# Another order of a period's small products, the mixing as 64x32 parts, and longer instruction periods, in a fused attention and feed-forward kernel

## The chip, the cores and the metric

The kernel runs on one core of one Trainium2 chip. The metric is device time in microseconds of one execution. Single executions of the kernel before agree within 0.25 us (1237.48 to 1237.73). A profiled execution gives the trace that is read here; its times are counted from the start of its span. L12 is line 12 of the kernel. The engines are TensorE (PE, its weight loads PEld), VectorE (DVE), ScalarE (ACT), GpSimd (POOL) and SyncE (SP), which issues most of the DMA transfers.

## What is computed

The input x is 128 sequences of 32 positions with 512 channels. All of it is float32. Cut to what matters:

```python
# 1. mixing: each sequence has its own 32x32 matrix, drawn from 16, that mixes its positions
h = einsum('bct,bcd->bdt', x, W[condition])
# 2. attention: clip, layer norm with affine on q and k, 32 heads of 16, ALiBi, causal
q, k, v = split(clip(h @ w_qkv.T, -8, 8))
q, k = layer_norm(q) * q_w + q_b, layer_norm(k) * k_w + k_b
s = where(causal, q @ k.T * 16**-0.5 + slopes * rel, -inf)
x = x + (softmax(s) @ v) @ w_out.T
# 3. adapters: each sequence has its own 512x512 matrix, drawn from 8
a = einsum('bsi,boi->bso', x, weight[adapter_ids])
# 4. feed-forward with a routed branch, layer norm, residual
shared = relu(a @ up) ** 2 @ down
routed = ((a @ fc1) @ expert) * sum(top2(a @ gate)) @ fc2
x = x + layer_norm(shared + routed) * gamma + beta
```

## The kernel before

The 4096 rows are cut into 32 tiles of 128 rows, which are four sequences. Every tile passes through a chain of steps that stretches over several periods; a loop over t, from 2 to 33, runs one period per turn and works on several tiles at once (L775 to L826). Two tiles make a pair, and the up product of the feed-forward is done for a pair: even t runs the eight blocks of up for pair t/2 - 1, odd t runs the eight quarters of down for the pair's two tiles. What stands before the loop (L662 to L767) brings tiles 0 to 3 to where the loop takes them up.

The steps that matter here, by the tile's name in the profile:

- mix (pxc, L290): the mixing. The four 32x32 matrices of a tile stand on the diagonal of a 128x128 block matrix blk, zero elsewhere (blend, L278); four products of 128x128 with 128 columns give xcT, channels by rows, copied out of the bank by ScalarE (L295).
- project (pqkv, L307): three products of 128 rows with 512 columns, for q, k, v.
- turn and scale: q and k are transposed. For tiles 0 to 3 TensorE does it (pt, L365); from tile 4 on VectorE transposes 32x32 blocks (L346), and DMAs through DRAM finish the swap (T_qk). ScalarE then applies the affine to the keys (L386) and to the queries (L400); VectorE makes kx, the keys of each head with zeros for the other heads (L390).
- scores (psc, L414): 32 products that use 64 rows and 32 columns of the array, 128 columns wide, into two banks; VectorE adds the bias (L424) and takes the maximum mx (L435), POOL subtracts it (L436), ScalarE exponentiates (L441).
- share and flip: VectorE sums (den, L446), POOL divides (L449), VectorE transposes (pT, L457).
- weigh (po, L484): the weighted values, 32 products that use 128 rows and 32 columns of the array, 64 columns wide; VectorE transposes the result (aT, L495).
- attend (pw, L506) applies the output matrix; turn_x transposes the new x (T_x), by the same kind of swap.
- adapt (pad, L536): the adapters, 64 products of 128 rows and 32 columns of the array, 128 columns wide; VectorE transposes the result into hT (L541), the input of up and of the routed branch (route, pr, L555).
- up and down (pu, pd, L104), each up block followed by a relu on ScalarE (L585) and a square on POOL (L586).

A float32 product appears in the trace as two records of weight load and two of matmul. So a tile's scores are 64 matmul records, its adapters 128, its mixing 8, its weighted values 64.

Order. TensorE's instructions run in the order of the loop's text: weigh(t), adapt(t - 1), scores(t + 1), route, mix(t + 2), then the projections of t + 2 and the blocks of up or down between them. `after(a, b)` (L77) only orders two instructions of one engine; in adapt and scores it keeps the scores behind the last adapter product. The other engines' instructions are ordered by when the planner of the language expects their inputs, except where `after` fixes it.

Fillers. `fill(i)` (L779) emits block i of up or down and behind it `fill_up(n)`, which emits n empty instructions (NOPs) on TensorE, held between that block and the next product of up or down. n comes from FIRST (t = 2) and SHORT (even t, odd t), spread over the eight blocks: 116 at t = 2, 7 in an even period, 71 in an odd one. In the program's text the products of an even period are 752 instructions (a product counts four), of an odd one 688; with the fillers and 9 semaphore instructions each makes 768.

SyncE's queue. `load_adapters(t)` (L239) issues eight loads of adapter weights; the first of them waits for the cue it is given, the maximum mx of tile t + 1. Behind it on SP stand the load of x for tile t + 3 and the swaps of q, k and x.

Memory. The pool of PSUM has eight banks, handed out in turn; T_qk, T_x, kx, s, pT and aT have one buffer each, xcT, vx and blk two (vx two halves), the adapter weights eight buffers, which is one tile's.

## Time and profile before

| what | value |
|---|---|
| median of three executions | 1237.62 us |
| the profiled execution | 1237.27 us |
| its span | 1235.5 us |
| mean granted TensorE clock | 0.999 |
| DMA traffic | 209.31 MB, mean 169 GB/s |

| one period from tile 16's weighted values on (607.06 us) | us from start to start |
|---|---|
| even period, t = 16 | 37.77 |
| odd period, t = 17 | 37.69 |

| the larger groups | records | busy us | mean ns |
|---|---|---|---|
| pqkv, 128x512 | 768 | 340.3 | 592 |
| pu, 128x256 | 1024 | 228.7 | 379 |
| pd, 128x512 | 496 | 220.4 | 592 |
| pad, 128x128 in 128*32 | 4096 | 118.4 | 273 |
| psc, 64x128 in 64*32 | 2048 | 37.2 | 274 |
| po, 128x64 in 128*32 | 2048 | 35.2 | 220 |
| pxc, 128x128 in 128*128 | 256 | 33.8 | 275 |

How to read it: matmul records overlap each other, and their ends are modelled, so a record's mean length is not what it adds to the time; the distance from one group's first start to the next group's is. Form 64*32 means that a record uses 64 rows and 32 columns of the array, so that eight such parts fit beside each other. A row of the timeline gives the start, the length of the merged stretch, the engine, the line, the operation, the names, the form and the number of records; in brackets, where there was idle time before it, its length and what ended it.

### The profile page before, as it was taken

The page shows a single profiled execution, that of the slowest core. Times are in us where ns is not written, and L with a number is a line of the kernel's source. Part 1 is how long each engine was busy: PE and PEld are TensorE (multiplying, and loading weights), DVE is VectorE, ACT ScalarE, POOL GpSimd, SP SyncE. Part 2 cuts the span into 40 slices and gives each one's busy share as a digit, 9 for nine tenths or more (in the row PEclk, how much of TensorE's full clock was granted, in tenths as well). Part 3 has the DMA queues.
Part 4 walks back from the last instruction along what each step waited for, and adds up shares of the span by engine and source line. Part 5 has one row for each costly group of instructions (what it writes and reads, how often), then busy time and mean ns, then how long its engine had stood idle before and what let it go on. Part 6 is the DMA issues. An engine that isn't in the chain of part 4 may idle for free.

```text
span 1235.5 us, 29216 instructions
## 1 busy us (share of the span) xinstructions
PE 1227.2 (99%) x11614; PEld 790.5 (64%) x11614; DVE 658.3 (53%) x1090; ACT 327.6 (27%) x648; POOL 431.5 (35%) x393
## 2 busy tenths in 40 slices
PE   9999999999999999999999999999999999999998
PEld 4577466675666756567665666746667566675765
DVE  2975655646456464563646546465564645646222
ACT  2432223222222313133222232222322222231211
POOL 4543333433423424334243333333333242332410
PEclk9999999999999999999999999999999999999999
DMA  9745553435545345544355543455443554434630
GB/s 289 220 166 197 206 205 147 156 121 196 205 174 177 102 175 197 200 162 140 139 185 206 184 155 125 155 206 205 150 154 124 190 204 176 176 110 157 209 116 18
DMA packets 93417, 209.31 MB, mean 169 GB/s; under 512 B 11749, under 2 KB 42470, under 8 KB 93286
## 3 DMA queue, kind: packets, MB, share of 16 engines
q1 hardware_dynamic: 89142, 198.39, 45.8%
q0 software_dynamic: 3424, 8.39, 1.9%
q8 instruction: 97, 1.59, 0.5%
q10 hardware_dynamic: 720, 0.66, 0.2%
q14 instruction: 34, 0.28, 0.1%
HBM read 176.47 MB, written 30.93 MB: 168 GB/s over the span
## 4 chain that ended last, share of the span: by engine, by line
PE 99%; DMA 0%; DVE 0%; ACTq 0%; issue 0%; DVEq 0%
PE pqkv L307 27%; PE pu L104 18%; PE pd L104 17%; PE pr L555 10%; PE pad L536 9%; PE pw L506 9%; PE psc L414 3%; PE po L484 3%; PE pxc L290 2%; PE pro L207 1%; PE pd L636 1%; DMA fc_t<-in_fc_w 0%; PE pt L365 0%; PE pe L197 0%; PE pt_x L365 0%; ACTq L124 0%
## 5 line engine op out<-in xcount | busy, mean ns | idle before, releaser
L307 PE MATMUL pqkv<-wqkv_sb,xcT 128*128 128x512 f32 x768 | 340.3, 592 | 0.0
L307 PEld LDWEIGHTS pqkv<-wqkv_sb,xcT 128*128 128x128 f32 x768 | 145.5, 190 | 168.6 <-issue 162.8
L104 PE MATMUL pu<-hT,up_sb 128*128 128x256 f32 x1024 | 228.7, 379 | 0.0
L104 PE MATMUL pd<-down_sb,act 128*128 128x512 f32 x496 | 220.4, 592 | 0.0
L104 PEld LDWEIGHTS pu<-hT,up_sb 128*128 128x128 f32 x1024 | 193.5, 190 | 32.6 <-issue 6.9
L390 DVE TENSOR_TENSOR kx<-T_qk,m_half 128x512 f32<-128x512 f32 x128 | 110.4, 920 | 102.7 <-ACT T_qk L386 102.7
L104 PEld LDWEIGHTS pd<-down_sb,act 128*128 128x128 f32 x496 | 93.2, 190 | 104.7 <-issue 103.6
L471 POOL TENSOR_TENSOR vx<-v,msk 128x1024 f32<-128x1024 f32 x64 | 127.2, 2010 | 56.6 <-DVE v L313 49.9
L586 POOL TENSOR_TENSOR act<-act 128x256 f32<-128x256 f32 x128 | 77.9, 614 | 168.6 <-ACT act L585 168.6
L555 PE MATMUL pr<-rout_sb,hT 128*128 128x256 f32 (+1 forms) x512 | 125.8, 389 | 0.0
L536 PE MATMUL pad<-adw,T_x 128*32 128x128 f32 x4096 | 118.4, 273 | 0.1
L555 PEld LDWEIGHTS pr<-rout_sb,hT 128*128 128x128 f32 x512 | 94.7, 190 | 32.1 <-issue 19.9
L506 PE MATMUL pw<-wout_sb,aT 128*128 128x512 f32 x256 | 115.2, 592 | 0.0
L536 PEld LDWEIGHTS pad<-adw,T_x 128*32 128x32 f32 x4096 | 110.7, 110 | 2.0 <-issue 1.2
L436 POOL TENSOR_TENSOR s<-s,mx 128x1024 f32<-128x1024 f32 x32 | 61.7, 1928 | 143.4 <-DVE top L562 141.8
L446 DVE TENSOR_REDUCE den<-s 128x32 f32<-128x1024 f32 x32 | 39.0, 1220 | 100.5 <-ACT s L441 100.5
L520 POOL TENSOR_TENSOR x<-x,bet_sb 128x512 f32<-128x512 f32 x32 | 40.7, 1272 | 147.1 <-DVE blocks_x L346 144.8
L506 PEld LDWEIGHTS pw<-wout_sb,aT 128*128 128x128 f32 x256 | 48.6, 190 | 60.6 <-issue 60.0
L585 ACT ACTIVATE act<-pu 128x256 f32<-128x256 f32 x128 | 47.2, 379 | 139.6 <-PE pu L104 139.6
L623 POOL DMA_DIRECT2D out<-y x30 | 18.0, 599 | 179.8 <-DVE y L619 93.1
L449 POOL TENSOR_TENSOR s<-s,rden 128x1024 f32<-128x1024 f32 x32 | 61.4, 1919 | 51.2 <-DVE rden L448 48.3
L295 ACT COPY xcT<-pxc 128x512 f32<-128x512 f32 x32 | 18.8, 586 | 201.8 <-PE pxc L290 201.8
(76 smaller groups left out, 1094.5 us busy)
## 6 DMA issues: line engine op xcount, KB each, us to landing
adw<-in_adapt_w SPq DMA_DIRECT2D x256, 512.0 KB, 7.5
away_qk<-blocks_qk SPq DMA_DIRECT2D x28, 512.0 KB, 2.6
T_qk<-away_qk SPq DMA_DIRECT2D x112, 128.0 KB, 2.9
x<-in_x SPq DMA_DIRECT2D x32, 256.0 KB, 9.3
away_x<-blocks_x SPq DMA_DIRECT2D x30, 256.0 KB, 2.7
T_x<-away_x SPq DMA_DIRECT2D x120, 64.0 KB, 2.4
out<-y POOLq DMA_DIRECT2D x30, 256.0 KB, 2.7
wqkv_sb<-in_w_qkvT SPq DMA_DIRECT2D x12, 256.0 KB, 5.3
```

What stands on the lines that cost most here:

```text
L104: ins = nc.tensor.matmul(*args, **kwargs)
L307: nc.tensor.matmul(s["pp", i], lhsT=s["xcT"][:, c, :], rhs=wqkv_sb[:, c, ts(i, D)], start=(c == 0), stop=(c == DC - 1),)
L390: kx = nc.vector.tensor_tensor(out=s["kx"][:, c], in0=k[:, :, c].unsqueeze(2).broadcast_to([P, SEQ, HQ, S]), in1=m_half.unsqueeze(1).unsqu ...
L436: nc.gpsimd.tensor_tensor(out=s["s"], in0=s["s"], in1=mx.unsqueeze(2).broadcast_to([P, H, S]), op=ALU.subtract,)
L449: nc.gpsimd.tensor_tensor(out=s["s"], in0=s["s"], in1=rden.unsqueeze(2).broadcast_to([P, H, S]), op=ALU.mult)
L471: nc.gpsimd.tensor_tensor(out=vx, in0=s["v"][:, ts(half, D // 2)].rearrange("p (h d) -> p h d", d=HD).unsqueeze(2) .broadcast_to([P, H // ...
L506: nc.tensor.matmul(pw, lhsT=s["aT"][:, g].rearrange("p b q -> p (b q)"), rhs=wout_sb[:, g, :], start=(g == 0), stop=(g == 3),)
L520: nc.gpsimd.tensor_tensor(out=s["x"], in0=s["x"], in1=bet_sb, op=ALU.add)
L536: last_pad[:] = [nc.tensor.matmul(pad[ts(g, S), ts(j, P)], lhsT=s["xT"][:, j, c], rhs=s["adw"][c // 2][j][:, c % 2, ts(g, P)], start=(c == ...
L555: nc.tensor.matmul(pr[:, :n], lhsT=hT[:, c, ts(t % GRP, P)], rhs=rout_sb[:, c, ROUT[half] : ROUT[half + 1]], start=(c == 0), stop=(c == DC ...
L585: nc.scalar.activation(a, pu[:, : GRP * P], AF.Relu)
L586: nc.gpsimd.tensor_tensor(out=a, in0=a, in1=a, op=ALU.mult)
```

## The change

- The order of the small products at a period's start becomes scores(t + 1), mix(t + 2), adapt(t - 1), weigh(t). A helper `short` issues them and holds each behind the one before with `after`.
- For tiles from 4 on the mixing is cut: only the two 64x64 diagonal halves of blk are used, as 32 products of 64 rows, 32 columns of the array and 64 columns of data, into two banks, one for each half of the rows; ScalarE copies the two halves of xcT out in two instructions. Tiles 0 to 3 are mixed as before.
- The fillers: FIRST is 3, SHORT is (152, 214), spread over the first seven blocks; behind the eighth there are none.
- In the fifth block of up, the relu is ordered behind the last scaling of the queries (`last_scale`), which stands behind that of the keys on ScalarE.
- The sum den of tile t + 1 is ordered behind the last transposition of the small products on VectorE (`last_head`: aT, or hT at t = 2), and the adapter loads take that transposition as their cue in place of mx.

```diff
--- before.py
+++ after.py
@@ -35,8 +35,8 @@
 ROUT = (0, NE + D // 2, NE + D)
 
 
-SHORT = (7, 71)
-FIRST = 116
+SHORT = (152, 214)
+FIRST = 3
 CLIP = 8.0
 EPS = 1e-5
 NEG = -1.0e30
@@ -92,6 +92,7 @@
 
 
     queue = []
+    shorts = []
 
     def fill_up(n):
 
@@ -104,6 +105,14 @@
         ins = nc.tensor.matmul(*args, **kwargs)
         if queue:
             after(ins, queue.pop())
+        return ins
+
+    def short(*args, **kwargs):
+
+        ins = product(*args, **kwargs)
+        if shorts:
+            after(ins, shorts[-1])
+        shorts[:] = [ins]
         return ins
 
 
@@ -285,14 +294,29 @@
     def mix(t):
 
         s = tiles[t]
-        pxc = bank(f"pxc_{t}")
+        s["xcT"] = w2.tile([P, DC, P], F32, tag="xcT", name=f"xcT_{t}")
+        blk = s["blk"].rearrange("p a b -> p (a b)")
+        if t < 2 * GRP:
+            pxc = bank(f"pxc_{t}")
+            for c in range(DC):
+                nc.tensor.matmul(
+                    pxc[:, ts(c, P)], lhsT=s["x"][:, ts(c, P)], rhs=blk, start=True, stop=True
+                )
+            nc.scalar.copy(s["xcT"].rearrange("p c n -> p (c n)"), pxc)
+            return
+
+        n = P // 2
+        banks = [bank(f"pxc_{t}_{r}").rearrange("p (c n) -> p c n", c=DC) for r in range(2)]
         for c in range(DC):
-            nc.tensor.matmul(
-                pxc[:, ts(c, P)], lhsT=s["x"][:, ts(c, P)],
-                rhs=s["blk"].rearrange("p a b -> p (a b)"), start=True, stop=True,
-            )
-        s["xcT"] = w2.tile([P, DC, P], F32, tag="xcT", name=f"xcT_{t}")
-        nc.scalar.copy(s["xcT"].rearrange("p c n -> p (c n)"), pxc)
+            for g in range(DC):
+                for r in range(2):
+                    short(
+                        banks[r][ts(g, S), c, :n],
+                        lhsT=s["x"][ts(r, n), c * P + g * S : c * P + (g + 1) * S],
+                        rhs=blk[ts(r, n), ts(r, n)], start=True, stop=True,
+                    )
+        for r in range(2):
+            nc.scalar.copy(s["xcT"][:, :, ts(r, n)], banks[r][:, :, :n])
 
     def project(t, i, chunks=range(DC)):
 
@@ -334,7 +358,8 @@
                     after(add, done)
 
     last_flip = []
-    last_pad = []
+    last_head = []
+    last_scale = []
 
     def swap(srcs, name):
 
@@ -397,10 +422,10 @@
             if c == 0 and last_flip:
                 after(kx, last_flip[-1])
         for c in range(DC):
-            nc.scalar.activation(
+            last_scale[:] = [nc.scalar.activation(
                 q[:, :, c], s["raw"][0][:, :, c], AF.Identity,
                 bias=qaff[:, 1, c : c + 1], scale=qaff[:, 0, c : c + 1],
-            )
+            )]
 
     def scores(t):
 
@@ -411,14 +436,12 @@
             for b in range(SEQ):
                 for r in range(2):
                     rows_r = slice(r * P // 2, (r + 1) * P // 2)
-                    psc = nc.tensor.matmul(
+                    psc = short(
                         banks[r][ts(b, S), ts(c, HQ * S)],
                         lhsT=s["T"][rows_r, b, 0, c],
                         rhs=s["kx"][rows_r, c, b].rearrange("p h k -> p (h k)"),
                         start=True, stop=True,
                     )
-                    if last_pad:
-                        after(psc, last_pad.pop())
         s["psc"] = psc
         for r in range(2):
             add = nc.vector.tensor_tensor(
@@ -443,7 +466,9 @@
     def share(t):
         s = tiles[t]
         den = sm.tile([P, H], F32, tag="den", name=f"den_{t}")
-        nc.vector.tensor_reduce(out=den, in_=s["s"], axis=AX.X, op=ALU.add)
+        total = nc.vector.tensor_reduce(out=den, in_=s["s"], axis=AX.X, op=ALU.add)
+        if t > GRP:
+            after(total, last_head[-1])
         rden = sm.tile([P, H], F32, tag="rden", name=f"rden_{t}")
         nc.vector.reciprocal(rden, den)
         nc.gpsimd.tensor_tensor(
@@ -481,7 +506,7 @@
         s = tiles[t]
         po = bank(f"po_{t}")
         for h in range(H):
-            nc.tensor.matmul(
+            short(
                 po[ts(h % 4, S), :].rearrange(
                     "p (e b i d) -> p e i b d", e=DC, b=SEQ, d=HD
                 )[:, h // 8, h // 4 % 2],
@@ -495,6 +520,7 @@
         aT = nc.vector.transpose(
             out=s["aT"].rearrange("p e b q -> p (e b q)"), in_=po
         )
+        last_head[:] = [aT]
         if t == 0:
             after(tiles[2]["stats"], aT)
 
@@ -533,17 +559,17 @@
         for j in range(SEQ):
             for c in range(DC):
                 for g in range(DC):
-                    last_pad[:] = [nc.tensor.matmul(
+                    short(
                         pad[ts(g, S), ts(j, P)], lhsT=s["xT"][:, j, c],
                         rhs=s["adw"][c // 2][j][:, c % 2, ts(g, P)],
                         start=(c == 0), stop=(c == DC - 1),
-                    )]
-        nc.vector.transpose(
+                    )
+        last_head[:] = [nc.vector.transpose(
             out=pairs[t // GRP]["hT"][:, :, ts(t % GRP, P)].rearrange(
                 "p e (j n) -> p e j n", j=SEQ
             ),
             in_=pad.rearrange("p (j e d) -> p e j d", j=SEQ, d=S),
-        )
+        )]
 
     def route(t, half):
 
@@ -582,7 +608,10 @@
                 start=(c == 0), stop=(c == DC - 1),
             )
         a = hp.tile([P, GRP * P], F32, tag="act", name=f"act_{g}_{f}")
-        nc.scalar.activation(a, pu[:, : GRP * P], AF.Relu)
+        relu = nc.scalar.activation(a, pu[:, : GRP * P], AF.Relu)
+
+        if f == FC // 2 and last_scale:
+            after(relu, last_scale.pop())
         nc.gpsimd.tensor_tensor(out=a, in0=a, in1=a, op=ALU.mult)
         pair["acts"].append(a)
         return last
@@ -778,18 +807,19 @@
 
         def fill(i):
             last = up(g, i) if t % GRP == 0 else down(g * GRP + i // 4, i % 4)
-            short = FIRST if t == GRP else SHORT[t % GRP]
+            lack = FIRST if t == GRP else SHORT[t % GRP]
             queue[:] = [last]
-            fill_up(short // 8 + (i < short % 8))
-
+            fill_up(lack // 7 + (i < lack % 7) if i < 7 else 0)
+
+        when(ahead, scores, t + 1)
+        when(two, mix, t + 2)
+        when(t <= NTILE, adapt, t - 1)
         when(here and t > GRP, weigh, t)
-        when(t <= NTILE, adapt, t - 1)
-        when(ahead, scores, t + 1)
         when(ahead, exponent, t + 1)
         if here:
 
 
-            load_adapters(t, tiles[t + 1]["mx"] if ahead else None)
+            load_adapters(t, last_head[-1])
         if t == GRP:
             after(
                 nc.sync.dma_start(out=gam_sb, in_=gamma.broadcast_to([P, D])),
@@ -798,7 +828,6 @@
         when(t + 3 < NTILE, load, t + 3)
         when(t > GRP and t % GRP == 0, finish, t - GRP - 1)
         when(t > GRP, route, t - GRP, 0)
-        when(two, mix, t + 2)
         fill(0)
         when(two, project, t + 2, 0)
         when(ahead, share, t + 1)
```

## The prediction

> **What bounds it now.** I read the page's busy times first, then its chain of waits.
>
> ```profile
> PE 1227.2 (99%) x11614; PEld 790.5 (64%) x11614; DVE 658.3 (53%) x1090; ACT 327.6 (27%) x648; POOL 431.5 (35%) x393
> ...
> PE 99%; DMA 0%; DVE 0%; ACTq 0%; issue 0%; DVEq 0%
> ```
>
> TensorE runs without a hole and the chain never leaves it, so another engine matters only where it comes to be waited for. The time is the sum of what stands in TensorE's order, and a period is read as starts in its timeline. This is tile 16's head (weighted values, adapters, scores, routing, mixing, first block of up):
>
> ```profile
> 607.06 1.10 PE L484 MATMUL po<-vx,pT 128*32 128x64 f32 x64
> 607.98 3.69 PE L536 MATMUL pad<-adw,T_x 128*32 128x128 f32 x128
> 611.60 1.16 PE L414 MATMUL psc<-kx,T_qk 64*32 64x128 f32 x64
> 612.68 2.05 PE L555 MATMUL pr<-rout_sb,hT 128*128 128x264 f32 x8
> 614.57 1.05 PE L290 MATMUL pxc<-blk,x 128*128 128x128 f32 x8
> 615.46 1.89 PE L104 MATMUL pu<-hT,up_sb 128*128 128x256 f32 x8
> ```
>
> From start to start: 0.92, 3.62, 1.08, 1.89, 0.89, together 8.40 us. Everything behind the head (29.3 us, large products back to back) keeps its order.
>
> **The change, part by part.** Durations are of the profiled execution, 1237.27 us (span 1235.5 and 1.8 around it); the median shown, 1237.62, is 0.35 above it.
>
> *Mixing in parts.* Removed: 8 records of 128x128, 0.89 us. Added: 32 matmuls (64 records) of 64x32 with 64 columns. No row has this form, so it is bounded. Below: in the single records of psc, eight parts of the array start a record each per 0.107 us; half the columns would give 64/8 x 0.053 = 0.43. Above: as dear as psc's own, 1.08/64 = 17 ns each, 1.09 us. In between lies what I take. In psc's records the first eight matmuls load at 6.7 ns apart, but the seventeenth loads only 0.435 us after the first: 0.135 to the second record of the first matmul, 0.269 that record, 0.03 on. So sixteen are in flight. With half the columns the second record follows at 0.06, and po's 64-column record is 0.219 long: 0.31 per sixteen, 0.62 for 32, and 0.06 behind the last scores. I take 0.68.
>
> [...]
>
> *Order.* A change of the array's shape costs a drain: from psc's last record to pr's first load 0.20; from po's (64 columns) to the transposes in the prologue 0.15. Before, a head had a drain into po (outside the 8.40), 0.20 after pad and 0.20 after psc. Now it has the same drain into psc, none between psc and mixing, 0.15 after mixing, none between pad and po, 0.15 after po. The new head: psc 1.08 - 0.20 = 0.88; mixing 0.68 + 0.15; pad 3.50 (in the prologue, followed by its own shape, 64.40 to 67.92, 3.52); po 0.92 + 0.11 = 1.03; pr 1.89. Sum 8.13, or **0.27 us less per period**. The periods t = 3 to 29 have all parts: 27 x 0.27 = 7.3. Periods 30 and 31, without mixing, gain 0.05 each.
>
> *The first period.* At t = 2 the head had pad, psc, pxc, and pad covered the wait for tile 3's keys:
>
> ```profile
> 83.27 3.70 PE L536 MATMUL pad<-adw,T_x 128*32 128x128 f32 x128
> 86.90 1.16 PE L414 MATMUL psc<-kx,T_qk 64*32 64x128 f32 x64
> 87.98 1.16 PE L290 MATMUL pxc<-blk,x 128*128 128x128 f32 x8
> 88.98 1.89 PE L104 MATMUL pu<-hT,up_sb 128*128 128x256 f32 x8
> ```
>
> ```profile
> 84.19 2.50 DVE L390 TENSOR_TENSOR kx<-T_qk,m_half 128x512 f32<-128x512 f32 x4 [1.09 <-ACT T_qk L386]
> 87.04 0.72 DVE L541 STREAM_TRANSPOSE hT<-pad 128x512 f32<-128x512 f32 x1 [0.35 <-PE pad L536]
> ```
>
> Now scores come first and wait for kx, ready at 86.69; the chained mixing and adapters queue behind them. Last quarter of the scores 0.27, mixing 0.83, pad 3.63, hT 0.14 + 0.72, start of up 0.1: 92.4 instead of 88.98. The first up needs hT and nothing stands between them here, so this is **+3.3 us**, less perhaps 0.4 if the early scores are done by then. I take +3.0, once (2.0 to 3.6).
>
> *Edits at nothing.* Later the scores' new place needs kx at the period's start. For odd periods kx ended 1.7 us before the next start (680.85, from 676.65, against 682.52); for even ones it ended 0.1 after it, because two relus (L585) went ahead of the scalings:
>
> ```profile
> 639.76 0.38 ACT L585 ACTIVATE act<-pu 128x256 f32<-128x256 f32 x1 [1.25 <-PE pu L104]
> 641.48 0.38 ACT L585 ACTIVATE act<-pu 128x256 f32<-128x256 f32 x1 [1.34 <-PE pu L104]
> 641.76 1.64 ACT L386 ACTIVATE T_qk<-T_qk,lnc 128x128 f32<-128x128 f32 x4
> 643.30 1.64 ACT L400 ACTIVATE T_qk<-T_qk,qaff 128x128 f32<-128x128 f32 x4
> ```
>
> The new order on ACT holds the fifth relu behind the last scaling. The keys can then start after y (638.51) and end near 641.6, kx near 643, 1.9 before 644.83. Behind the held relu wait the later relus, their squares on POOL and pu's banks, each wanted only by the next period. Cover gone, each late microsecond is paid per period. Two ACT copies (0.38 each, by act's row of the same width) replace one of 0.59; xcT is wanted 7 us later. The weight loads now wait on SP for aT or hT (about 7 us into the period) instead of mx (8.3); x's load stands behind them there, and the next adapters start 30 us later, eight issues (4.9 us) and 7.5 to land. den on DVE waits for aT; pT is wanted a period later. hT still has po, the drain and pr (2.9 us) before up.
>
> *Fillers.* In the records they are 71 ns apart, executed while TensorE has some 33 instructions before it. Even periods get 22 behind each of seven blocks, 1.56 us against the block's 1.73. Odd ones get 30 or 31, 2.2 us against 1.72; the three in a row (91 x 0.071 = 6.5) run against 33 instructions (5.4 us) and two blocks (3.4): 2.4 us stay in hand. Cost nothing; with no lead at all, 3 x 0.45 us per odd half.
>
> Sum: -7.3 - 0.1 + 3.0 = -4.4 on 1237.27, with 0.35 for the median: 1233.2. A part of a tenth per period for waits of the mixing's own (its bank, its data) I leave in: 27 x 0.02. **1233.7.**
>
> **Rivals.** *Blocks of instructions in the way (slower).* TensorE's stream comes in 16 KB packets:
>
> ```profile
> q8 instruction: 97, 1.59, 0.5%
> ```
>
> 24,840 instructions (loads, records, 1322 fillers, 290 semaphores) over 97 are 256 each. Before, a period was three blocks; by counting, boundaries fell ahead of po, inside pad, and at the end of psc, none of which shows a gap. A boundary in the middle of scores does: tile 2's in the prologue.
>
> ```profile
> 68.92 1.35 PE L414 MATMUL psc<-kx,T_qk 64*32 64x128 f32 x64
> 70.20 3.70 PE L307 MATMUL pqkv<-wqkv_sb,xcT 128*128 128x512 f32 x8
> ```
>
> 1.28 instead of 1.08, with 0.12 us without a record in the middle, though kx was long there. Now 640 instructions pass in 6.2 us and, counted from t = 2 (707 and a few semaphores), boundaries fall at the start of scores, at the end of mixing, at the end of pad. The middle one is where little is queued ahead, with 0.15 of drain to hide it. If a stop of 0.2 to 0.5 shows there, a period changes by -0.07 to +0.23; it decides for slower from 0.27 - 3.0/27 = 0.16 on. At 0.45: 27 x 0.18 + 3.0, or 1245.4. For it: the gap above. Against: boundaries 3.1 us apart (inside pad, end of psc) cost nothing, and these are 3 to 4.5 apart. [...]
>
> *Parts at the array's rate (faster).* Mixing 0.43, pad 3.45: -0.57 a period, -15.4 + 2.9: 1225.1. For it: single starts 7 ns apart. Against: the 0.435 turnaround.
>
> *Late scores.* If kx misses the start by 1 us in every odd period: +13, 1247. Against: 1.7 us in hand.
>
> *No effect.* Parts as dear as psc's (1.09): +0.14 a period, 1244; between that and the forecast, gain and first stop cancel, 1237.
>
> **Numbers.** Forecast 0.42 (own range 1229 to 1236.5); array's rate 0.20; blocks in the way 0.22; parts too dear or cancelling 0.11; late scores 0.05. A measurement tells 0.2% (2.5 us) from no change: below 1235.1 lie 0.34 of the forecast's and all of the array's, 0.54; above 1240.1 the blocks' 0.17, late 0.05, dear 0.05, 0.27; the rest 0.19. The range: low end 1226 (most of the array's case), high end 1245 (blocks at 0.45, dear parts).
>
> **What would show it.** psc to pad start 1.7 us in every period, pad 3.5, po 1.0, no drain between psc and mixing; a hole of about 1.6 us before tile 3's scores at 83 us and another before the first up; period length 37.4 to 37.5 instead of 37.77 and 37.70. It is wrong if the stretch from psc to pad exceeds 1.95, if PE idles before psc, or if records are missing at the end of mixing.

## The result and the profile after

The changed kernel takes 1257.62 us (median of four, 1254.08 to 1259.23), the one before beside it 1237.55: a ratio of 1.016, 95% interval 1.0137 to 1.0183. It is slower by 20 us; the forecast was 1233.7, in a range of 1226 to 1245. The profiled execution took 1254.08, 16.8 above that of before (1237.27). The page:

```profile
PE 1226.5 (98%) x13182; PEld 790.0 (63%) x13182; DVE 684.9 (55%) x1090; ACT 331.4 (26%) x676; POOL 462.4 (37%) x393
...
q8 instruction: 126, 2.06, 0.7%
...
PE 97%; issue 1%; DMA 0%; DVE 0%; ACT 0%; ACTq 0%; DVEq 0%
```

TensorE is busy for as long as before (1227.2) in a span 16.5 us longer, and "issue", which was 0%, is 1% of the chain: the new time is time in which TensorE waited for nothing that the profile shows. The list of its waits, with total, count and longest, says where:

```profile
PE pad L105 <- issue: 14.1, 10, 1.7
PE psc L105 <- DVE kx L415: 1.8, 2, 1.6
...
PE pu L105 <- DVE hT L567: 0.8, 1, 0.8
```

Ten times, in the adapters. Here are two heads of TensorE's timeline (start, length, line, group, count), an odd one, t = 17, and the even one ahead of it, t = 16:

```profile
653.75 1.16 PE L105 MATMUL psc<-kx,T_qk 64*32 64x128 f32 x64
654.64 0.91 PE L105 MATMUL pxc<-blk,x 64*32 64x64 f32 x64
655.48 3.70 PE L105 MATMUL pad<-adw,T_x 128*32 128x128 f32 x128
659.00 1.11 PE L105 MATMUL po<-vx,pT 128*32 128x64 f32 x64
660.04 2.05 PE L581 MATMUL pr<-rout_sb,hT 128*128 128x264 f32 x8
```

```profile
613.99 1.16 PE L105 MATMUL psc<-kx,T_qk 64*32 64x128 f32 x64
614.88 0.91 PE L105 MATMUL pxc<-blk,x 64*32 64x64 f32 x64
615.72 0.42 PE L105 MATMUL pad<-adw,T_x 128*32 128x128 f32 x7
617.81 3.57 PE L105 MATMUL pad<-adw,T_x 128*32 128x128 f32 x121 [1.67 <-issue]
621.11 1.46 PE L105 MATMUL po<-vx,pT 128*32 128x64 f32 x64
```

From start to start the odd head is 0.89, 0.84, 3.52, 1.04 and (to the next group) 1.89, which is 8.18 us; before it was 8.40. The even head is the same up to the seventh record of the adapters. Then nothing runs for 1.67 us. From one record's start to the next it is 1.94 us (1.4 to 1.9 in the ten heads), where two records of the adapters otherwise start 0.03 apart. In this head the weighted values behind it lose another 0.35. Undisturbed periods take 37.43 (odd) and 37.51 (even) against 37.69 and 37.77; in ten of the thirteen even periods from t = 4 to 28 the period takes 39.0 to 39.8. The odd ones never have the hole.

The sum: 27 periods at -0.26 are -7.0; the first period is 3.6 longer (from tile 2's weighted values to the head of t = 3, 39.01 us against 35.41); the holes and what follows them, period by period over the undisturbed length, add 19.6. That makes 16.2 of the 16.8 (the rest lies in the prologue, at the end and outside the span). Other executions, up to 1259, would fit one to three more holes. The first period, t = 2, reads as foretold: the scores wait for the keys, and the first up for hT.

```profile
85.42 1.05 PE L105 MATMUL psc<-kx,T_qk 64*32 64x128 f32 x32 [1.60 <-DVE kx L415]
86.71 1.05 PE L105 MATMUL psc<-kx,T_qk 64*32 64x128 f32 x32 [0.24 <-DVE kx L415]
...
88.38 3.77 PE L105 MATMUL pad<-adw,T_x 128*32 128x128 f32 x128
92.96 0.48 PE L105 MATMUL pu<-hT,up_sb 128*128 128x256 f32 x1 [0.81 <-DVE hT L567]
```

What is the hole? The queue q8 fetched 126 packets, each of 16,384 bytes in the trace, for TensorE's 32,274 instructions there (loads, records, 5617 fillers, 290 semaphores, three more): 256 to a packet, as in the kernel before (24,843 over 97). Where a boundary between two such blocks lies can be counted: the scores are 128 instructions (four for a product) and four semaphores, the mixing 128 and two, and 7 records into the adapters are 14 more: 276. So a block ends 276 instructions behind the start of the scores, and the one before it ended at 20. Every period has 1024 instructions, so it lies there in all. The trace has a record of each fetch, 0.9 to 1.5 us long; against the start of the scores (in the kernel before: of the weighted values, which stood first there), the fetches of a head begin at (us, medians):

```
head                                        first   second  third
before, odd periods                         -2.4    +3.0    +7.7
before, even periods                        -4.7    +3.1    +8.1
after, odd periods                          -2.4    +2.7    +6.4
after, even, the three without a hole       -3.3    +2.8    +6.4
after, even, the ten with a hole            +1.2    +4.8    +8.2
```

Where there is a hole the first fetch is 4.5 us late. Fetches in this trace follow each other by 3.3 us at least. In the head above the late one begins 1.59 us behind the start, takes 0.96, and the adapters go on at 3.82. So in the ten heads a block whose fetch began only 1.1 to 1.6 us behind the start of the scores was run from 3.3 to 3.8 us behind it, and the block in hand, 256 instructions of scores and mixing, was run down at 1.9.

The trace shows when a fetch begins, not what sets it off. The theory (A) was: the boundary just behind the start of the scores is noticed too late. Rivals: the 64x32 parts or the new order stop the array by themselves (B); the fillers eat the sequencer's lead (C).

### The profile page after: what moved, and what is told of

Read it like the earlier page. It is cut to its first block, busy times and chain, and to the rows that moved or that the text cites. A ratio compares the mean times of both kernels' runs of the same rounds, so it can differ in the third digit from the quotient of the medians.

```text
span 1252.0 us, 36640 instructions
## 1 busy us (share of the span) xinstructions
PE 1226.5 (98%) x13182; PEld 790.0 (63%) x13182; DVE 684.9 (55%) x1090; ACT 331.4 (26%) x676; POOL 462.4 (37%) x393
## 4 chain that ended last, share of the span: by engine, by line
PE 97%; issue 1%; DMA 0%; DVE 0%; ACT 0%; ACTq 0%; DVEq 0%
PE pqkv L331 26%; PE pu L105 18%; PE pd L105 17%; PE pad L105 9%; PE pr L581 9%; PE pw L532 9%; PE psc L105 3%; PE po L105 2%; PE pxc L105 2%; PE pro L216 1%; PE pd L665 1%; DMA fc_t<-in_fc_w 0%; PE pxc L302 0%; PE pt L390 0%; DVE kx L415 0%
## 5 line engine op out<-in xcount | busy, mean ns | idle before, releaser
L415 DVE TENSOR_TENSOR kx<-T_qk,m_half 128x512 f32<-128x512 f32 x128 | 138.8, 1143 | 55.3 <-ACT T_qk L411 55.3
L615 POOL TENSOR_TENSOR act<-act 128x256 f32<-128x256 f32 x128 | 89.8, 710 | 190.7 <-ACT act L611 190.7
L496 POOL TENSOR_TENSOR vx<-v,msk 128x1024 f32<-128x1024 f32 x64 | 134.8, 2129 | 56.7 <-DVE v L337 50.0
L105 PE MATMUL pad<-adw,T_x 128*32 128x128 f32 x4096 | 121.7, 274 | 14.2 <-issue 14.1
L337 DVE TENSOR_SCALAR qk<-pqkv 128x512 f32<-128x512 f32 x64 | 44.1, 690 | 90.5 <-PE pqkv L331 90.3
L459 POOL TENSOR_TENSOR s<-s,mx 128x1024 f32<-128x1024 f32 x32 | 67.8, 2119 | 42.1 <-DVE mx L458 41.9
L482 DVE STREAM_TRANSPOSE pT<-s 128x1024 f32<-128x1024 f32 x32 | 39.8, 1245 | 61.8 <-POOL s L474 61.8
L225 ACT ACTIVATE std_f<-mvf,eps 128x1 f32<-128x1 f32 x32 | 9.4, 295 | 218.3 <-DVE mvf L638 211.0
```

What stands on the lines that cost most here:

```text
L105: ins = nc.tensor.matmul(*args, **kwargs)
L337: nc.vector.tensor_scalar(out=s["qk"][:, i, :] if i < 2 else s["v"], in0=s["pp", i], scalar1=-CLIP, scalar2=CLIP, op0=ALU.max, op1=ALU.min,)
L415: kx = nc.vector.tensor_tensor(out=s["kx"][:, c], in0=k[:, :, c].unsqueeze(2).broadcast_to([P, SEQ, HQ, S]), in1=m_half.unsqueeze(1).unsqu ...
L459: nc.gpsimd.tensor_tensor(out=s["s"], in0=s["s"], in1=mx.unsqueeze(2).broadcast_to([P, H, S]), op=ALU.subtract,)
L496: nc.gpsimd.tensor_tensor(out=vx, in0=s["v"][:, ts(half, D // 2)].rearrange("p (h d) -> p h d", d=HD).unsqueeze(2) .broadcast_to([P, H // ...
L615: nc.gpsimd.tensor_tensor(out=a, in0=a, in1=a, op=ALU.mult)
```

## The experiments

**Moving the boundaries, nothing else.** FIRST sets how many empty instructions stand in the period t = 2, and so where the boundaries lie in all later ones.

```diff
-FIRST = 3
+FIRST = 19      # e1;  131 in e2;  239 in e14
```

> 16 more fillers in the first period, so every later block boundary lies 16 instructions earlier in the code: just ahead of the scores instead of just behind their start. Theory A (a block of instructions asked for too late: the boundary behind the start of the scores is reached only when they start, and the block after it is run down in 1.9 us while a new block takes about 3.4): the sequencer crosses the boundary before it is stopped ahead of the scores, the hole of 1.4 to 1.9 us in the adapters is gone in all ten periods that had it, even and odd periods are 37.5 and 37.4 us; 10 x 2.0 less: 1234 to 1236 us. Rival B (the 64x32 parts or the new order of the head themselves cost the stop, by the array or a bank): no change, 1254 to 1259.

> 128 more fillers in the first period: boundaries about 110 instructions ahead of the scores, in the mixing (about 150 behind the start of the scores) and in the middle of the adapters (about 400). Theory A: the second and third are passed about 1.0 and 3.7 us after the start, 2.7 us apart where a block takes 3.4: a stop of 0.5 to 0.7 us in the adapters or a little before, in nearly every period, even and odd: 1245 to 1255; if the sequencer's lead covers it, 1235. The long hole 7 records into the adapters is gone in either case. Rival B: no change, 1254 to 1259, hole at the same record.

Measured: e1 1242.69 us (ratio to before 1.0046, 1.0033 to 1.0059), e2 1254.79 (1.0146, 1.0132 to 1.0161). A late head of e1 (t = 6):

```profile
234.12 1.16 PE L105 MATMUL psc<-kx,T_qk 64*32 64x128 f32 x64
235.02 0.91 PE L105 MATMUL pxc<-blk,x 64*32 64x64 f32 x64
237.76 3.72 PE L105 MATMUL pad<-adw,T_x 128*32 128x128 f32 x128 [1.83 <-issue]
```

Sixteen instructions more in t = 2, and the hole is seven records earlier, behind the last part of the mixing: the new boundary, to the instruction. It ends at the same time, 3.64 us behind the start, and so is longer. Only three even heads are late instead of ten; I had expected none. Eight periods lose 0.2 to 0.6 behind record 127 of the adapters, the next boundary. In e2 no head is late, and each one stops 0.5 to 0.9 us (start to start) at record 71, its boundary: two boundaries are passed there 2.8 us apart, and no two fetches of the changed kernel's trace are closer than 3.3. Its head at t = 8, from 312.19 on:

```profile
313.92 2.17 PE L105 MATMUL pad<-adw,T_x 128*32 128x128 f32 x71
316.68 1.82 PE L105 MATMUL pad<-adw,T_x 128*32 128x128 f32 x57 [0.59 <-issue]
```

B is out for the long hole: the same parts in the same order run without it.

> The changed kernel with 236 more fillers in the first period: boundaries 40 instructions behind the start of the scores, past the second semaphore there, which the sequencer passes 0.02 us behind the start in every head. Theory (the hold at the semaphores makes the late request): every head of 3 to 30 is late, odd ones too, first block fetched 1.1 to 1.4 us behind the start, the hole at the 17th record of the adapters, 1.1 to 1.5 us long: 27 x 1.2 to 1.6 on 1235: 1265 to 1280. Rival (lateness has to do with the even periods or comes at random): holes in the even ones or fewer, 1250 to 1260.

Measured: 1288.36 (1.0413, 1.0397 to 1.0429). All 27 heads are late, odd ones too. The odd head t = 5, and the line of the waits:

```profile
200.93 1.16 PE L105 MATMUL psc<-kx,T_qk 64*32 64x128 f32 x64
201.83 0.91 PE L105 MATMUL pxc<-blk,x 64*32 64x64 f32 x64
202.67 0.73 PE L105 MATMUL pad<-adw,T_x 128*32 128x128 f32 x17
204.76 3.15 PE L105 MATMUL pad<-adw,T_x 128*32 128x128 f32 x108 [1.35 <-issue]
```

```profile
PE pad L105 <- issue: 33.3, 27, 1.5
```

Record 17, as counted, and again up to 3.83 us behind the start. (The time is above the 1265 to 1280 expected; in 18 heads the weighted values wait too, 5.3 us in all.) The scores carry semaphores, 4 and 33 instructions behind their start. In the changed kernel's trace TensorE's sequencer passes the first about 4.3 us (even) or 3.5 us (odd) ahead of the scores from t = 4 on, and the second 0.02 us behind their start, in every head of both sorts. In the head above the second was open by then: it waits for a part of kx, and all of kx was ready at 199.63, 1.3 us ahead of the scores.

```profile
195.02 4.61 DVE L415 TENSOR_TENSOR kx<-T_qk,m_half 128x512 f32<-128x512 f32 x4 [1.92 <-ACT T_qk L411]
```

In the changed kernel its record is 0.05 us long in every head, where one that really waits, in e10 below, is 2.17. So what keeps the sequencer from it is rather its lead, which the prediction read off the fillers as some 33 instructions: by this reading a boundary 40 behind the start lies beyond that and is reached only when the scores run. The changed kernel's, at 20, lies within it, so e14 shows what a late fetch costs and not why the changed kernel's is late.

**The lead, and the semaphore.** e7 is the changed kernel with

```diff
-            fill_up(lack // 7 + (i < lack % 7) if i < 7 else 0)
+            fill_up(lack // 5 + (i < lack % 5) if i < 5 else 0)
```

> The changed kernel with its fillers behind the first five large blocks of a half instead of the first seven; periods, boundaries and everything else as there. Rival C (the late first block comes of the fillers just ahead of the head, which use up the sequencer's lead in the odd periods, so that it reaches the boundary late): no hole in the even periods, 1235 to 1238, perhaps 0.5 us lost where 43 fillers stand behind three blocks in a row. Theory A' (the place of the boundary behind the scores' semaphores alone decides): holes as in the changed kernel, 1252 to 1259.

Measured: 1254.89 (1.0137, 1.0121 to 1.0152), with eight holes at the same record, all in even heads. C is out.

e10 is e8 of the table below without the hold of the relu (and with one more filler in the odd periods, SHORT = (152, 215)):

```diff
-        if f == FC // 2 and last_scale:
-            after(relu, last_scale.pop())
```

> As the first of these (boundaries 4 ahead of the scores), without the order that holds the fifth relu behind the scalings, so two relus go ahead of the keys' affine again. The keys' products then end about 0.2 us behind the start of the scores in odd periods instead of 1.7 ahead, and the last quarter of the scores is wanted only 0.67 behind it. Theory: costs nothing, same as the first within 1 us. Rival (the prediction's late scores): each late 0.1 to 0.5 us is paid in 14 periods: 1.5 to 7 us more.

Measured: 1275.60 against 1246.52 for e8, the same kernel with the hold: +29, where I had expected nothing. ScalarE and TensorE in the odd head t = 7:

```profile
270.51 1.63 ACT L425 ACTIVATE T_qk<-T_qk,qaff 128x128 f32<-128x128 f32 x4
272.05 0.63 ACT L611 ACTIVATE act<-pu 128x256 f32<-128x256 f32 x2
```

```profile
272.03 1.16 PE L105 MATMUL psc<-kx,T_qk 64*32 64x128 f32 x64
272.93 0.87 PE L105 MATMUL pxc<-blk,x 64*32 64x64 f32 x60
274.64 0.30 PE L105 MATMUL pxc<-blk,x 64*32 64x64 f32 x4 [0.83 <-issue]
```

The scores start on time. But in the odd heads the sequencer now waits 2.17 us at a semaphore at their start and passes the next one 1.0 us ahead of them instead of 3.5, since the keys and the scalings come late. The fetch follows 1.0 us behind that or later, in seven heads at the start of the scores instead of 2.4 ahead, and 12 of 14 odd heads have holes of 0.8 to 1.8 us (start to start). The data was in time; the fetch of instructions was not. This supports A a second time, by moving the wait and not the boundary. It holds for some 20 of the 29 us; the rest is in the even heads (seven late, four in e8), which pass their semaphores as before, and is not explained.

**Order and parts apart.** e4 mixes whole again in the new order, with periods of three blocks (SHORT = (8, 71), FIRST = 114) and the first boundary where the changed kernel has it. e11 has the parts in the old order (and SHORT = (151, 214)).

> Mixing whole again (8 products of 128x128), in the new order of the head, periods of three blocks with the first boundary at the same place behind the start of the scores as in the changed kernel. Theory A: from the first to the second boundary the head now takes 0.9 + 0.9 + 1.6 us of adapters, 3.4, so at most 0.1 us of stop; the head costs 1.08 + 1.05 + 3.51 + 1.03 + 1.88 = 8.55 against 8.40 in the kernel before, 0.0 to 0.15 more a period, and 3.3 more in the first: 1240 to 1245. Rival B1 (the order causes the hole, whatever the boundaries): the hole of 1.4 to 1.9 us stays in the even periods, 1257 or more. Rival B2 (the parts cause it): no hole, as theory A here; the shift alone tells A from B2.

> The mixing in parts, but the head in the order of before (weighted values, adapters, scores, routing, mixing), periods of four blocks, first boundary where before and the changed kernel have it, behind the start of the head's first group. Forecast: 0.92 + 3.62 + 1.09 + 1.88 + 0.1 + 0.83 = 8.44 against 8.40: the parts need their neighbours' shape to gain. No semaphores stand ahead of the boundary in the weighted values, boundaries are passed 3.0 and 7.3 us in: no late block. 1237 to 1240. Rival (the parts themselves cost the stop): 1250 or more. If the parts gain by themselves: 1232 or less.

```diff
+        when(here and t > GRP, weigh, t)
+        when(t <= NTILE, adapt, t - 1)
         when(ahead, scores, t + 1)
-        when(two, mix, t + 2)
-        when(t <= NTILE, adapt, t - 1)
-        when(here and t > GRP, weigh, t)
...
+        when(two, mix, t + 2)
         fill(0)
```

Measured: e4 1255.97 (1.0149, 1.0134 to 1.0163), e11 1246.97 (1.0078, 1.0064 to 1.0093); both above what was expected. An even head of e4 (t = 8):

```profile
312.44 1.16 PE L105 MATMUL psc<-kx,T_qk 64*32 64x128 f32 x64
313.53 1.16 PE L302 MATMUL pxc<-blk,x 128*128 128x128 f32 x8
314.62 3.91 PE L105 MATMUL pad<-adw,T_x 128*32 128x128 f32 x128
318.26 1.11 PE L105 MATMUL po<-vx,pT 128*32 128x64 f32 x63
320.21 0.24 PE L105 MATMUL po<-vx,pT 128*32 128x64 f32 x1 [0.85 <-issue]
```

The first fetch is late here too, in 10 of 13 even heads, with no part in the kernel. But whole mixing lets the block in hand last to 3.9 us, and only the third boundary, one record from the end of the weighted values, costs 0.2 to 1.1. In e11, with the parts and the boundary at the same distance behind the head's first group, no head is late. Its first group, the weighted values, has its semaphores at the end; that this is the reason was not tested. So **with the new order the fetch came late, and the parts made the lateness expensive**. Undisturbed, the order alone adds 0.18 us a period (37.87 and 37.95), the parts alone 0.09 in even periods, and both together take 0.26 off: here the parts paid only beside groups of their own shape. e11's odd periods (38.22) lose another 0.44; the runs with a long product, further down, bear on that.

**A place for the boundaries, and t = 2.** In the following the first period has the adapters ahead of the scores, as before the change:

```diff
+        when(t == GRP, adapt, t - 1)
         when(ahead, scores, t + 1)
         when(two, mix, t + 2)
-        when(t <= NTILE, adapt, t - 1)
+        when(GRP < t <= NTILE, adapt, t - 1)
```

FIRST is 19 in e3 and 63 in e5. e8 and e9 also mix tile 4 whole, which takes 96 instructions out of that period (FIRST 139 and 145):

```diff
-        if t < 2 * GRP:
+        if t <= 2 * GRP:
```

> As the kernel with 16 more fillers, and in the first period the adapters go ahead of the scores again, as in the kernel before. Forecast: the first period loses the wait for tile 3's keys and for its own hT, 3.0 to 3.5 us less than the kernel with 16 more fillers alone: 1231 to 1232 if theory A is right, 1251 to 1256 if B is. Rival: the wait only moves (the first scores of the loop are late anyway): same as that kernel.

> Adapters ahead of the scores in the first period, and 60 more fillers there than in the changed kernel: the first boundary then lies about 40 instructions ahead of the scores, before their semaphores, the second about 216 behind their start (inside the mixing, 1.4 us), the third about 472 (inside the adapters, 4.7 us). Theory A with 'the late request comes from a boundary just behind the semaphores at the start of the scores': no late first block in any period; but the second block has 3.3 us where a block takes 3.4 and its fetch 0.9 to 1.5, so delays of 0.1 to 0.4 us in the adapters in many periods: 1233 to 1238, and less spread than the shift by 16. If the late request has another cause (fillers, keys), late first blocks remain in some even periods: 1238 or more.

> Adapters first and tile 4's mixing whole in the first period, boundaries about 4 instructions ahead of the scores, just before their first semaphore. The second is then in the last parts of the mixing (1.7 us), the third about 508 behind the start (5.1 us). Theory A: no late first block, and the third block has 3.6 us instead of the 3.3 of the shift by 60, so fewer delays in the adapters: about 0.1 a period on the average against 0.25. No late block in the first period, 0.4 less. 1233 to 1236, against 1239 for the shift by 60. Rival: the boundary is so near the first semaphore that late first blocks of about 2 us come back in some even periods: 1237 to 1245.

> As the one before, boundaries 6 instructions earlier (about 10 ahead of the scores). Theory A: delays between those of the two shifts, 1233.5 to 1237; no late first block even if the other has some.

| run | first boundary against the scores | late heads, t = 3 to 29 (even, odd) | median us | ratio, 95% |
|---|---|---|---|---|
| after | 20 behind | 10, 0 | 1257.62 | 1.0137 to 1.0183 |
| e1 | 4 behind | 3, 0 | 1242.69 | 1.0033 to 1.0059 |
| e3 (t = 2 as before) | 4 behind | 2, 0 | 1240.93 | 1.0019 to 1.0048 |
| e8 (also tile 4 mixed whole) | 4 ahead | 4, 0 | 1246.52 | 1.0061 to 1.0091 |
| e9 (as e8) | 10 ahead | 6, 0 | 1254.07 | 1.0121 to 1.0161 |
| e5 (t = 2 as before) | 40 ahead | 0, 0 | 1238.95 | 1.0004 to 1.0022 |

The heads are counted in one profiled execution each; e3's eleven runs reach from 1237.5 to 1247.9, so the number seems to change from run to run. The adapters' old place at t = 2 takes about 3 us off: from the prologue's scores to t = 3 it is 82.9 us in e3 and 85.9 in the changed kernel. With the boundary 40 ahead no head is late, and what is left in e5 is 0 to 0.6 us a period behind record 105 of the adapters, its third boundary: the second and third are passed 3.2 us apart, a little less than the 3.3 between the closest fetches of the changed kernel's trace. e8 and e9 missed: 4 and 10 instructions ahead of the scores were still too near. In them, and in e10, the boundary lies ahead of the scores and of the semaphores named above, and heads are late all the same. So it looks as if the fetch is set off not at the boundary but some way behind it. How far isn't shown; 10 ahead was too near, and 24 and 40 ahead were not (e16 below, and e5).

**A long product between the short ones.** e6 is e5 with the routing's half between mixing and adapters, so that 16 instructions take 1.9 us there:

```diff
         when(two, mix, t + 2)
+        when(t > GRP and t % GRP == 0, finish, t - GRP - 1)
+        when(t > GRP, route, t - GRP, 0)
         when(GRP < t <= NTILE, adapt, t - 1)
...
-        when(t > GRP and t % GRP == 0, finish, t - GRP - 1)
-        when(t > GRP, route, t - GRP, 0)
```

e12 also mixes tile 4 whole and puts only 8 fillers behind the first block. e13 instead moves `project(t + 1, 2)` to that place.

> As the kernel before this one, and the routing's half (8 long products, 1.88 us for 16 instructions) stands between the mixing and the adapters instead of behind the weighted values. The changes of the array's shape stay the same in number. Boundaries are then passed 1.4 and 6.3 us after the start of the scores, 4.9 us apart. Theory A: no delay left by blocks anywhere in the loop, periods 37.4 and 37.5 throughout: 1230 to 1232, spread under 2 us. Rival: hT is only 1.0 us ahead of the first up in even periods (0.14 + 0.72 + 0.1), and a wait of up to 0.1 shows there: 1231 to 1233. If another thing than the blocks delays the adapters, they keep their 0.1 to 0.5: 1234 or more.

> As the kernel with the routing's half between mixing and adapters (1245), with tile 4's mixing whole in the first period and the odd and even periods' fillers moved off the first large block, which now follows the weighted values directly: 8 stand there, the rest behind the next six. Theory: the 0.2 to 0.34 us ahead of the queries' product in odd periods were the fillers (31 x 0.071 = 2.2 us against 1.72 of the block, with no lead left behind 128 short instructions); gone now: odd periods 37.55 to 37.65 instead of 38.06, even ones 37.72 as there, first period 0.6 less: 1237 to 1240. Rival (the wait is for data: den's place behind the weighted values' transposition): 38.06 stays, 1244.

> As the changed kernel with the adapters first and tile 4's mixing whole in the first period, and the values' product of the next tile (8 long products, 3.43 us for 16 instructions) moved up between mixing and adapters; boundaries 40 instructions ahead of the scores. No block is passed in under 5 us in the head, so no delay by blocks; one more change of the array's shape (0.10, as ahead of the adapters behind the routing's half). Periods 37.53 and 37.61 against 37.69 and 37.77 before: 1232 to 1234. Rivals: a wait for a bank or for DVE's values in the new place, 0.1 to 0.3 a period: 1235 to 1241.

Measured: e6 1245.42 (1.0065, 1.0052 to 1.0079), e12 1237.36 (0.9998, 0.9989 to 1.0007), e13 1293.33 (1.0451, 1.0437 to 1.0465). In e6 and e12 no gap at a block boundary is left in the loop. The routing's half costs 0.1 for one more change of shape, and the block that follows the weighted values 0.1: even periods 37.72. e6's odd ones were 38.06: 31 fillers (2.2 us) behind a block of 1.72 that follows the weighted values, 128 short instructions, and by my estimate no lead left. The profile gives 2.8 us of these waits to den; but with den in the same place and 8 fillers there the odd periods are 37.63 (e12). e11 has 31 fillers in such a place too, and its odd periods are longer by as much; that it is the same was not run apart. e13 failed for another reason: the chain runs through kx again. With 3.4 us taken out of the middle of the period, kx stands on VectorE behind a sum (y) of the feed-forward, which waits for down, and the scores of t = 16, which could have started at 632.2, wait for it:

```profile
632.32 0.69 DVE L634 TENSOR_TENSOR y<-y,pd 128x512 f32<-128x512 f32 x1 [5.37 <-PE pd L105]
633.65 2.48 DVE L415 TENSOR_TENSOR kx<-T_qk,m_half 128x512 f32<-128x512 f32 x4
634.53 1.60 PE L105 MATMUL psc<-kx,T_qk 64*32 64x128 f32 x48 [2.31 <-issue]
```

**Once more on other chips.** e15 and e16 put the boundaries where no head should be late and the third block comes later (24 ahead of the scores; in e15, by SHORT = (108, 258), 20 behind in the odd periods).

> Adapters first and tile 4's mixing whole in the first period; fillers 108 and 258 instead of 152 and 214, so that boundaries lie 20 instructions behind the start of the scores in the odd periods (where the changed kernel lost nothing) and 24 ahead of it in the even ones. Theory: no late first block in either; odd periods 37.43 to 37.5; the third block of the even ones comes 0.1 to 0.3 us late on the average. 13 x 0.2 on 1231.5, 1233 to 1235.5, which beats both kernels. Rival (24 ahead is still too near the semaphores): 2 us in some even periods, 1237 to 1250; or the 258 fillers cost their lead: odd periods longer by 0.3 to 1, 1236 to 1246.

> The same, but boundaries 24 instructions ahead of the scores in all periods, fillers 152 and 214. Theory: no late first block, the third 0 to 0.4 us late in both halves, 0.15 to 0.2 on the average: 1235 to 1238. Rival (still too near): 1240 to 1250.

> e15's kernel a second time. If the gaps away from the boundaries were the chip's: 1233 to 1237, gaps only at the boundaries (record 7 and 113 of the adapters). If they are the kernel's: 1243 to 1245 again, gaps at records 64 and 77 to 83.

> The shift by 60 a second time, which had gaps only at record 104, its boundary, and 1239. If the chip of this run makes gaps away from the boundaries, they show here too and the time is 1243 or more; if not, 1238 to 1240.

Measured: e15 1243.59 and again (e17) 1242.36, e16 1245.14, and e5's kernel again (e18) 1243.83 instead of 1238.95. No head is late in any of them. But every period from t = 3 to 23, and none later, has a gap of 0.3 to 0.5 us, from one record's start to the next, inside the adapters, behind record 60 to 83. It ends 3.9 us (odd) or 4.35 (even) behind the start whatever the boundaries are. In e18's head t = 6, which starts at 230.99, it stands in the chain as a new start at 235.35, and POOL has its gather of the mixing's coefficients for a later tile ahead of it:

```profile
232.79 2.52 PE pad L105 x83
235.31 0.04 issue
235.35 1.39 PE pad L105 x42
```

```profile
234.04 1.01 POOL L238 DMA_INDIRECT cw<-in_cond_w,rows  x1 [0.27 <-POOL blk L287]
```

The gaps stand in just the periods that have such a gather, and end 1.3 us behind its start, in odd and even heads alike. But the same kernel had none of them in e5, on another chip, with the gathers at the same 2.6 us (odd) and 3.1 us (even) behind the start. So this is a coincidence in time, not a shown cause. The 21 periods of e17 are together 10.0 us longer than undisturbed ones; without that its profiled execution (1243.48) would stand near 1233.5, about what was expected of it; no run shows that.

## Why the prediction was wrong

**The head: right.** The forecast was psc 0.88, mixing 0.68 + 0.15, pad 3.50, po 1.03, pr 1.89; measured are 0.89, 0.84, 3.52, 1.01 to 1.04 and 1.88 to 1.89. An undisturbed period gained 0.26 against 0.27, and e4 and e11 bear out the reason given for it, the saved changes of shape. **The first period: right in kind**, +3.0 forecast (2.0 to 3.6), 3.6 measured; the adapters' place makes 3.1 of it (e3). The prediction's own terms for it add to 3.4, not 3.3. Without the holes the profiled execution would have come out near 1234.5.

**What failed is the price and the mechanism of the rival "Blocks of instructions in the way".** It was named, with 0.22 and 1245.4. The step that failed is "Against: boundaries 3.1 us apart (inside pad, end of psc) cost nothing, and these are 3 to 4.5 apart". It judged the boundaries by their distance from each other, as if every block were asked for in time. The stop came at the middle boundary, as the rival said, but it was set by the first, which was counted "at the start of scores" and then left out of the argument. In ten even periods the fetch that belongs to it began only 1.1 to 1.6 us behind the start of the scores; its block was run from 3.3 to 3.8 on, and the block in hand was run down at 1.9. So the stop was not 0.2 to 0.5 us in all periods, from the prologue's row, but 1.4 to 1.9 and what follows in ten of them: 19.6 us in all, 0.7 a period on the average. The prediction also misplaced the boundaries of before. By the count of instructions its "ahead of po" is 20 behind po's start, and its "end of psc" 12 into the routing. So before has a boundary at the same distance behind the head's start as the changed kernel, and there the fetch begins 2.4 to 4.7 us ahead (medians). What makes the difference is open as far as the changed kernel goes. With a wait of 2.17 us at the scores' start (e10), or a boundary 40 instructions behind it (e14), fetches were late, but in the changed kernel's even heads the traces show neither.

**Edits at nothing.** The fillers cost nothing in the changed kernel (odd periods 37.43); they did behind a block that followed short products (e6, and perhaps e11), which was the prediction's case of "no lead at all", 0.45 a block (38.06 against 37.63, 0.43). The relu hold was priced as cover for late data. Its larger worth is that the sequencer gets past the scores' first semaphores early: e10 has the scores on time and loses 29 us, some 20 of them in the odd heads. "Late scores" and "no effect" didn't happen. "Parts at the array's rate" fell: 0.69 us of start to start for the mixing and 0.15 behind it, not 0.43.

**Open.** Why the fetch is late in some even heads with a boundary from 20 behind to 10 ahead and, with the relu held, never in odd ones, in which the semaphores are passed as regularly; and the gaps of the last four runs. No version beat the kernel before: e12 equals it, and e5 is 0.1% slower (0.5% in e18).

## What to carry to other kernels

Count TensorE's instructions as well as its time. Where a few hundred short ones stand together, find the block boundaries and ask for each how early the sequencer can get past it. Where it waited at a semaphore when the group started (e10), or the boundary lay 40 instructions behind that start (e14), the late fetches cost holes of 0.8 to 1.8 us; and with the finer cut of the products the block in hand ran out at 1.9 us instead of 3.9 (e4). Here a gap that the profile gave to "issue" was such a boundary: it moved by seven records when 16 empty instructions were put into the first period (e1), the cheapest test of all.

## What the runs showed of the hardware

- A block of 256 instructions whose fetch began only when the scores ran was run from 3.3 to 4.2 us behind their start, at whatever record the hole began (after, e1, e9 and e14): 1.0 to 1.9 us to the fetch, 0.9 to 1.4 for it, and 1.2 to 1.6 more.
- The closest two fetches of TensorE's blocks were 3.36 us apart in the kernel before, 3.31 in the changed one and at least 3.25 in all runs (e3 and e7 come nearest), and 256 instructions of scores and mixing ran in 1.7 us (after).
- Beside groups of their own shape the 64x32 records with 64 columns start 11 ns apart in the mean (0.69 us for 64), those with 128 columns 14 ns (0.89 us for 64), both in the changed kernel's head at t = 17.
- The same kernel was 1238.95 us on one chip (e5) and 1243.83 on another (e18), with the kernel before at 1237.5 on both.
